# Seven chunks of a layer's matrix products by Strassen's seven products on one Trainium2 core

## The chip, the core and the metric

One NeuronCore of a Trainium2 chip runs the program. Its engines work side by side, each through its own queue in order: TensorE (PE) multiplies matrices into PSUM; VectorE (DVE) and ScalarE (ACT) read PSUM and SBUF; GpSimd (POOL) works on SBUF; SyncE (SP) starts the DMA transfers. They wait for each other through semaphores. The metric is the device time of one execution in microseconds, the median of several runs; lower is better.

## The reference

Two layers over `x` of shape (2, 2048, 512): a conditioned state-space block with a feed-forward part, then attention between two conditioned norms. What matters here, cut from the reference:

```python
# first layer
mod = t @ Wm + bm                      # six rows: shift, scale, gate, twice
y_mod = _ln(y) * (1 + scale_a[:, None]) + shift_a[:, None]
a_y = _s5(y_mod, ...)                  # in-projection, recurrence over L, out-projection
y = y + gate_a[:, None] * a_y
y_norm = _ln(y) * (1 + scale_c[:, None]) + shift_c[:, None]
y_mod = y_norm * (1 + scale_ff[:, None]) + shift_ff[:, None]
h = jax.nn.gelu(y_mod @ W1 + b1)       # 512 -> 2048
ff_y = h @ W2 + b2                     # 2048 -> 512
x = y + gate_ff[:, None] * ff_y
# second layer
h = _sln(x, ...)                       # conditioned layer norm
qkv = h @ Wqkv.T + bqkv                # 512 -> 3 * 512, 16 heads of 32
out = softmax(q k^T) / D**0.5 @ v
h1 = out @ Wp.T + bp + x
return _sln(h1, ...) + h1
```

All arithmetic is in float32.

## The kernel before

The 2 x 2048 rows are cut into eight chunks of 512 rows (`order`). A first stage turns every chunk into x, q, k and v for attention and stores these in DRAM (`x2`, `qd`, `kd`, `vd`); a second stage runs the attention, block by block, from there. Only the first stage is touched by the change, and its two ends.

The order of all work is written out by hand: the engines execute their instructions in the order in which the Python program issues them. For chunk `now` the loop over `f` (16 steps) issues `ff_first` (a block of 128 of the 2048 hidden columns: four float32 matmuls on 128x512 into one PSUM bank, then a gelu on ACT), and one step later `ff_second` (that hidden block times its rows of `w2`, into four accumulating banks, one for each 128 rows of the chunk). Other work is hung between these steps through the dictionary `due`: for the chunk `ahead` its norm (`normalised`), the turning into feature order by 32x32 blocks on DVE and sixteen small DMAs (`by_blocks`), the in-projection, recurrence and out-projection of the state-space block (`s5_in`, `s5_turn`, `s5_scan`, `s5_out`, `s5_direct`), and its second norm (`ff_norm`, `ff_features`); for the chunk `behind` its attention norm (`at_norm`, `at_features`), then q and k (`at_heads`, eight products of 128 columns each, stored in a high and a low half by `halves`) and v (`at_values`). `ff_out` gates the feed-forward's result and adds it to x. A norm is four rows of statistics on DVE (`ln_row`), a chain of twelve small DVE operations (`ln_scale` with `rsqrt`) and four normalising operations (`normalise`).

W1, W2 and the weights of q, k and v lie in SBUF throughout the stage (`w1_sb`, `w2_sb`, `wk`, `wq`, `wv`). PSUM: two single banks for small products (`ones`), two for `ph`, four for `po`. The v of the last two chunks, and q and k of the last, are computed at the start of the second stage (`left`).

## Time and profile before

| what | value |
|---|---|
| median of 3 runs | 3381.46 us (3381.16 to 3383.28) |
| span of the profiled execution | 3379.3 us |
| before the first feed-forward matmul | 0 to 65 us |
| first chunk | 65 to 201.6 us |
| six chunks, each with one ahead and one behind | 164.8 us each |
| last chunk | 137.3 us |
| attention and the end | from 1332.5 us |

The profile is of one execution. A line such as `L538 PE MATMUL ph<-fT,w_sb 128*128 128x512 f32 x1024` gives the line of the code (in a helper where one issues the work), the engine, the output and the inputs by their names, the shapes, how often it occurs, then busy time, mean duration of one and the idle time of the engine before it, with what ended most of that. A float32 matmul of the program appears as two records, for it takes two passes. PEld is the load of a matmul's stationary operand. A mean duration of a matmul includes its way through the array; where matmuls follow each other, the distance of their starts is what each costs. The granted clock (PEclk) is the share of TensorE's full speed.

### The profile page before, as it was taken

How to read it: one execution, taken by the hardware profiler on the slowest of the kernel's cores; microseconds unless marked ns; L12 is line 12 of the kernel's file. 1: busy time of each engine (PE TensorE's matmuls, PEld its weight loads, DVE VectorE, ACT ScalarE, POOL GpSimd, SP SyncE). 2: the span in 40 equal slices, each digit the busy share in tenths (PEclk: the TensorE clock that was granted, in tenths of full speed). 3: DMA queues.
4: the chain of work that ended last, by engine and by line, in shares of the span. 5: the costliest groups of instructions: out<-in, count | busy, mean ns of one | idle time of the engine just before them, and what ended most of it. 6: DMA issues, size and time to landing. Idle time of an engine off the chain costs nothing.

```text
span 3379.3 us, 33635 instructions
## 1 busy us (share of the span) xinstructions
PE 3286.6 (97%) x11076; PEld 1417.1 (42%) x11076; DVE 2218.1 (66%) x2792; ACT 1956.4 (58%) x2210; POOL 2110.7 (62%) x1166
## 2 busy tenths in 40 slices
PE   7999999999999999999999999999999999999996
PEld 4444444444444444444444444434444434444432
DVE  5352525252525211688888888888888888888884
ACT  2111111111111111599999999999889888988962
POOL 2341313131313111399999999989999999999886
PEclk9999999999999999999999999999999999999998
DMA  8022222222222212332313231323233343243233
GB/s 299 25 50 72 53 77 48 78 54 74 62 63 54 59 50 75 106 87 68 74 49 74 68 74 49 74 69 76 67 95 89 68 93 88 61 95 86 62 100 101
DMA packets 249781, 259.07 MB, mean 77 GB/s; under 512 B 94920, under 2 KB 167112, under 8 KB 245510
## 3 DMA queue, kind: packets, MB, share of 16 engines
q1 hardware_dynamic: 249606, 256.92, 29.1%
q8 instruction: 88, 1.44, 0.2%
q14 instruction: 87, 0.71, 0.1%
HBM read 166.77 MB, written 67.76 MB: 69 GB/s over the span
## 4 chain that ended last, share of the span: by engine, by line
PE 62%; ACT 17%; DVE 13%; issue 3%; DMA 2%; POOL 1%; SPq 1%; ACTq 0%; DVEq 0%; POOLq 0%
PE ph L538 13%; PE po L551 13%; PE o L925 10%; PE s L856 8%; DVE run L872 7%; ACT x L867 7%; PE pk L587 7%; ACT x L915 5%; ACT pT L915 4%; PE pv L599 3%; DVE pT L910 3%; PE py L1008 3%; DVE run L876 2%; PE pu L474 2%; PE pt_run L884 1%
## 5 line engine op out<-in xcount | busy, mean ns | idle before, releaser
L904 POOL TENSOR_TENSOR x<-x,shift 128x1024 f32<-128x1024 f32 x704 | 1653.1, 2392 | 131.9 <-DMA shift<-flat 117.0
L856 PE MATMUL s<-qs,ks 128*128 128x512 f32 x2688 | 823.4, 427 | 38.0 <-DVE run L872 25.5
L867 ACT COPY x<-s 128x1024 f32<-128x1024 f32 x704 | 692.0, 1011 | 142.7 <-PE s L856 134.5
L872 DVE TENSOR_TENSOR run<-s,run 128x1024 f32<-128x1024 f32 x576 | 705.0, 1224 | 76.3 <-ACT x L867 31.3
L915 ACT ACTIVATE x<-x 128x1024 f32<-128x1024 f32 x704 | 737.7, 1058 | 18.5 <-POOL x L904 18.2
L925 PE MATMUL o<-x,v 128*64 128x512 f32 x2816 | 717.4, 611 | 0.0
L856 PEld LDWEIGHTS s<-qs,ks 128*128 128x128 f32 x2688 | 444.4, 189 | 452.5 <-DVE run L872 157.2
L538 PE MATMUL ph<-fT,w_sb 128*128 128x512 f32 x1024 | 459.4, 592 | 0.9 <-ACT fT L682 0.9
L551 PE MATMUL po<-w_sb,hid 128*128 128x512 f32 x1024 | 460.0, 592 | 0.0
L542 ACT ACTIVATE hid<-ph,vec 128x512 f32<-128x512 f32 x128 | 87.8, 686 | 615.7 <-PE ph L538 615.7
L910 DVE TENSOR_TENSOR pT<-s,shift 128x1024 f32<-128x1024 f32 x320 | 388.6, 1215 | 51.6 <-PE s L856 51.3
L876 DVE TENSOR_TENSOR run<-s,run 128x1024 f32<-128x1024 f32 x320 | 389.0, 1216 | 9.5 <-PE s L856 9.0
L915 ACT ACTIVATE pT<-pT 128x1024 f32<-128x1024 f32 x320 | 339.4, 1061 | 76.5 <-DVE pT L910 76.1
L561 POOL TENSOR_TENSOR x<-x,gated 128x512 f32<-128x512 f32 x32 | 39.6, 1267 | 506.5 <-DVE gated L560 506.5
L925 PE MATMUL o<-pT,v 128*64 128x512 f32 x1280 | 329.2, 593 | 6.6 <-ACT pT L915 6.6
L164 DVE SCALAR_TENSOR_TENSOR lo<-pk,vec,hi 128x512 fp32r<-128x512 f32 x64 | 47.8, 746 | 422.9 <-ACT hi L163 422.9
L551 PEld LDWEIGHTS po<-w_sb,hid 128*128 128x128 f32 x1024 | 194.5, 190 | 243.9 <-issue 243.4
L538 PEld LDWEIGHTS ph<-fT,w_sb 128*128 128x128 f32 x1024 | 194.1, 190 | 243.3 <-issue 239.1
L925 PEld LDWEIGHTS o<-x,v 128*64 128x64 f32 x2816 | 157.2, 135 | 309.4 <-issue 251.2
L163 ACT ACTIVATE hi<-pk,vec 128x512 fp32r<-128x512 f32 x64 | 44.0, 687 | 373.3 <-PE pk L587 373.3
L524 POOL TENSOR_TENSOR x<-x,gated 128x512 f32<-128x512 f32 x28 | 35.4, 1265 | 255.2 <-DVE gated L523 255.2
L925 PEld LDWEIGHTS o<-pT,v 128*64 128x64 f32 x1280 | 91.4, 137 | 191.3 <-issue 142.5
(281 smaller groups left out, 2446.4 us busy)
## 6 DMA issues: line engine op xcount, KB each, us to landing
ks<-kd SPq DMA_DIRECT2D x128, 256.0 KB
qs<-qd SPq DMA_DIRECT2D x512, 64.0 KB
shift<-flat SPq DMA_DIRECT2D x64, 512.0 KB
moved<-fT SPq DMA_DIRECT2D x224, 64.0 KB
x<-in_x SPq DMA_DIRECT2D x8, 1024.0 KB
w_sb<-in_w SPq DMA_DIRECT2D x8, 1024.0 KB
kd<-hi SPq DMA_DIRECT2D x32, 256.0 KB
kd<-lo SPq DMA_DIRECT2D x32, 256.0 KB
```

Of the source, the lines that this page charges most:

```text
L538: nc.tensor.matmul(ph, w1_sb[:, k, f * P : (f + 1) * P], fts[b, c][:, k, :], start=k == 0, stop=k == KC - 1)
L551: nc.tensor.matmul(pos[b, c][:, t, :], hid[:, t * P : (t + 1) * P], w2_sb[:, f, :], start=f == 0, stop=f == FC - 1,)
L587: nc.tensor.matmul(pk, w[:, k, g * P : (g + 1) * P], hT[:, k, :], start=k == 0, stop=k == KC - 1)
L599: nc.tensor.matmul(pv, fts[b, c][:, k, t * P : (t + 1) * P], wv[:, k, :], start=k == 0, stop=k == KC - 1)
L856: nc.tensor.matmul(s[:, e, :], kst[pair_of[n], e][:, kt * P : (kt + 1) * P], qst[n][:, e, :], start=True, stop=True,)
L867: nc.scalar.copy(x, s)
L872: nc.vector.tensor_tensor(runs[n], s, kept[n, 0] if kt == 1 else runs[n], ALU.max)
L876: nc.vector.tensor_tensor(runs[n], raw_scores(n, kt), runs[n], ALU.max)
L904: nc.gpsimd.tensor_tensor(x, x, shifts[n], ALU.add)
L910: nc.vector.tensor_tensor(x, s, shifts[n], ALU.add)
L915: nc.scalar.activation(x, x, AF.Exp)
L925: nc.tensor.matmul(outs[n][64 * e : 64 * e + 64, :], v[:, kt, e : e + 2, :], x[:, e, :], start=first, stop=final,)
```

## The change

Chunk 0 is computed as before. For chunks 1 to 7 the products of feed-forward (both), of q and k, and of v (chunks 0 to 5, one step behind) are computed by Strassen's scheme in Winograd's form: both operands are cut into 2 x 2 blocks, seven products of blocks take the place of eight, with four sums of blocks of the weights, four of the activations and seven additions of the products.

The weight sums are made during chunk 0 on POOL (`combine`, four operations for each of 22 pieces, each on 128x256) and stored in DRAM with the original blocks that are needed (`w1d`, `w2d`, `wkd`, `wvd`). From then on the weights are streamed: `more` starts the load of the next tile of about 1 MB into a ring of four slots, whose first three are the places of `wk`, `wq` and `wv`. W1 loses its place in SBUF after chunk 0; W2's becomes that of the hidden activations `h1` and `h2`. At the end of the stage the weights of q, k and v are loaded again.

Two procedures issue the products, on 256 moving columns each. `pairs_of` makes the first feed-forward product (eight steps) and q and k (four steps); each step uses one PSUM tile `pp` of two banks, of which there are three:

```python
product(c, ws[c], 0, x11, 0, True, False)
product(c, ws[c], 1, t2, 1, False, False)
product(c, ws[c], 4, t4, 2, True, False)
product(c, ws[c], 2, t1, 3, False, False)
nc.scalar.copy(za[:, 0, :], pps[c][:, 0, :HC])
nc.vector.tensor_tensor(za[:, 0, :], pps[c][:, 0, HC:], za[:, 0, :], ALU.add)
if c:
    product(c - 1, ws.pop(c - 1), 6, x22, 3, False, True)
    more()
    nc.vector.tensor_tensor(za[:, 0, :], pp[:, 1, HC:], za[:, 0, :], ALU.add)
    take(c - 1, 0, 1, za[:, 0, :])
for what, *args in beside.get(2 * c, ()):
    what(*args)
product(c, ws[c], 3, x21, 0, False, True)
product(c, ws[c], 5, t3, 1, True, True)
nc.vector.tensor_tensor(za[:, 1, :], pp[:, 0, HC:], za[:, 0, :], ALU.add)
nc.vector.tensor_tensor(zb, pp[:, 1, :]..., za[:, 1:2, :].to_broadcast([P, 2, HC]), ALU.add)
take(c, 0, 0, pp[:, 0, :HC])
take(c, 1, None, zb...)
for what, *args in beside.get(2 * c + 1, ()):
    what(*args)
```

`whole_of` makes the second feed-forward product (depth 8) and v (depth 2), with two such tiles:

```python
product(0, pa[:, 0, :], True, False)
nc.scalar.copy(u, pa[:, 0, :])
run(0)
product(1, pa[:, 1, :], True, True)
run(1)
nc.vector.tensor_tensor(u, pa[:, 1, :], u, ALU.add)
product(2, pb[:, 1, :], True, False)
run(2)
product(3, pa[:, 0, :], False, True)
run(3)
take(0, 0, pa[:, 0, :])
product(5, pa[:, 1, :], True, True)
run(5)
nc.vector.tensor_tensor(v, pa[:, 1, :], u, ALU.add)
nc.vector.tensor_tensor(z, pb[:, 1, :], v, ALU.add)
take(1, 1, z)
product(4, pb[:, 0, :], True, True)
run(4)
nc.vector.tensor_tensor(v, pb[:, 0, :], v, ALU.add)
take(1, 0, v)
product(6, pb[:, 1, :], False, True)
nc.vector.tensor_tensor(u, pb[:, 1, :], u, ALU.add)
run(6)
take(0, 1, u)
```

`take` hands a finished quarter on: `hidden` (gelu on ACT, and on POOL the sums for the next product), `gated_in` (the first quarter is gated on DVE, the others on POOL, all are added to x on POOL), `heads` (the high and low halves, stored), `values_in` (bias, stored). `beside` and `run` hang the other work between the products, in place of `due`. For the two chunks around it this is, in `pairs_of` for feed-forward:

```python
beside[0] += rows[:2]           # norm of the chunk ahead
beside[1] += rows[2:3]
beside[2] += rows[3:]
beside[3] += scale
beside[4] += to[:2]
beside[5] += to[2:3]
beside[6] += to[3:] + turns[:1]
beside[7] += turns[1:2]
beside[8] += turns[2:] + move
beside[8] += [(s5_direct, *ahead)]
beside[13] += [(s5_features, *ahead, k) for k in range(KC)]
beside[10] += b_rows[:1]        # norm of the chunk behind
beside[11] += b_rows[1:2]
beside[12] += b_rows[2:3]
beside[13] += b_rows[3:]
beside[14] += b_scale
```

`s5_in` and `s5_turn` follow; then in `whole_of`:

```python
beside[0] += [(third,)]
beside[0] += [(s5_scan, *ahead)]
beside[1] += b_to + [(at_rows, *behind)] + b_turns + b_move
beside[2] += [(s5_out, *ahead, t)]            # for each t
beside[3] += [(fourth, 0), (fourth, 1)]
beside[3] += [(at_features, *behind, k) for k in range(KC)]
beside[3] += [(load_x, *order[i + 2])]
beside[3] += rows + scale
beside[5] += to + [(bias, t) for t in range(TT)]
beside[4] += turns + move
beside[4] += [(at_sums, *behind)]
```

`third` (POOL) and `fourth` (DVE) make the last two sums of the hidden activations, `at_sums` (POOL) those for q, k and v, `ff_sums` (DVE) those for the next chunk's first product, at the end of the chunk. In chunk 0 the jobs that make the weight sums stand two to a step from step 3 on; the first three loads of the ring stand at step 13. The accumulator's four banks and `ph`'s two become the three tiles `pp` after chunk 0.

## The prediction

> **What bounds the kernel now.** I read the page's totals and its 40 slices first, then busy time by stretch, then TensorE in order of time, then the groups by shape.

> ```profile
> span 3379.3 us, 33635 instructions
> ...
> PE 3286.6 (97%) x11076; PEld 1417.1 (42%) x11076; DVE 2218.1 (66%) x2792; ACT 1956.4 (58%) x2210; POOL 2110.7 (62%) x1166
> ...
> PEclk9999999999999999999999999999999999999998
> ```

> TensorE is busy nearly throughout, at full clock. The changed stage is slices 3 to 16. Busy time by stretch (start:end, length, then busy us of PE, PEld, DVE, ACT, POOL, granted clock, DMA share, GB/s), the second chunk and the last:

> ```profile
> 201.60:366.40 164.80, 164.80 (x385) 72.88 (x384) 64.27 (x116) 24.92 (x36) 42.97 (x32) 1.00 0.24 64
> ...
> 1195.20:1332.50 137.30, 137.30 (x321) 60.80 (x320) 19.79 (x40) 19.30 (x28) 10.42 (x8) 1.00 0.24 61
> ```

> PE has no gap at all: here a chunk's time is its number of matmul passes times their pitch. The pitch, from the timeline of PE (start, duration, engine, line):

> ```profile
> 390.64 3.60 PE L538 MATMUL ph<-fT,w_sb 128*128 128x512 f32 x8
> 394.08 3.60 PE L551 MATMUL po<-w_sb,hid 128*128 128x512 f32 x8
> ```

> Eight passes in 3.434 us: 0.4292 us for 512 columns. A float32 matmul of the program is two passes; 384 passes make 164.8 us. What shorter passes cost, from the groups by shape:

> ```profile
> L648 PE MATMUL pa_s<-direct,fT 128*128 128x128 f32 x16 | 1.9, 275 | 0.0
> ...
> L1164 PE MATMUL turned<-raw,w 128*128 128x256 f32 x4 | 1.0, 379 | 0.0
> ```

> At 256 columns (1.0 - 0.379)/3 = 0.207, half of 0.4292 is 0.2146: I take 0.215. At 128 columns 1.9/16 = 0.119, each with a weight load of its own, so the load recorded as 190 ns does not hold up a 256-column pass. [...]

> **The change part by part.** *Arithmetic.* A chunk's passes go from 128 + 128 (feed-forward) + 64 (q, k) + 32 (v) = 352 of 512 columns to 224 + 224 + 112 + 56 = 616 of 256: 151.1 - 132.4 = 18.7 us less, for six chunks. In the last chunk, without v, 137.3 - 120.4 = 16.9. In all 129 us, if PE stays gapless.

> *New waits.* It does not. In the built order of the changed program a PSUM pair of banks counts as one tile: a matmul into one bank waits for the last reader of the other. PE is in order, so every product behind it stands too. Durations of what it waits for:

> ```profile
> L137 DVE BATCH_NORM_STATS2 ln_st<-x 128x6 f32<-128x512 f32 x88 | 58.5, 664 | 0.0
> ...
> L126 DVE SCALAR_TENSOR_TENSOR rstd<-rs_b,rstd 128x4 f32<-128x4 f32 x66 | 23.7, 359 | 2.3
> ...
> L560 DVE TENSOR_TENSOR gated<-po,gate_f 128x512 f32<-128x512 f32 x32 | 21.4, 689 | 68.0 <-PE po L551 57.5 <-POOL x L561 10.5
> ...
> L497 DVE TENSOR_TENSOR m<-m,t_im 128x512 f32<-128x512 f32 x7 | 12.2, 1749 | 0.0
> ...
> L484 DVE TENSOR_TENSOR m<-m,m 128x512 f32<-128x512 f32 x7 | 4.8, 682 | 0.0
> ```

> and of ACT, L421 (801 ns) and the copies L604 (585 ns at 512 columns) and L867 (1011 at 1024). By these slopes a 256-column DVE add from PSUM is 0.42, an ACT copy 0.37, a gelu 0.48 (estimates); results follow the last pass by 592 - 429 = 0.16; a hand-over is 0.05. Per chunk:

> - First pairs (eight steps of 28 passes): the product into bank 0 waits for copy and add, 0.16 + 0.37 + 0.42 + 0.15 = 1.1, of which the previous step's last product (0.86) covers all but 0.24: 1.1 + 7 x 0.24 = 2.8. In the last step the copy stands behind four L421 (3.2), about 2.2 net. There too the twelve small operations of a norm's scale (2.35 us from 168.05 to 170.4, where POOL rests; 3.95 by their means, such as L126) stand before the last adds: 2 for them, 2 for add, add and gelu: 4.0. Sum 9.0.
> - Second product (32 passes each): after product 0 an ACT copy, 0.85. Product 5 waits for the gating multiply, which stands on DVE behind the second half of a 128x1024 subtraction (1.2, of which the wait is product 3's end), four norm rows (3.2, as from 85.4 to 88.6) and the scale (2.35): with the multiply and hand-over 7.6; with POOL busy 9.6. Product 4 waits for two adds, 1.6; product 6 for one, 0.95. Sum 11.0.
> - q and k pairs: 1.8 likewise and 2.4 at the end. v, four waits of the second kind, 0.85 + 0.95 + 1.7 + 0.95. Sum 8.7.
> - The next chunk's sums stand behind v's last add on DVE: 0.16 + 0.69 + two at 0.68 (1.7 beside POOL, L497 against L484) less the product that needs none, 0.86: 2.4.
> - Restarts: some 25 a chunk at 0.1 (the first pair of passes after a wait took 1.12 against 1.02). After a gap of 5.9 us at 55 us the clock was 0.58 over the next 5, and sixteen transposes took 3.68 instead of 1.95: so about 2 for the 7.6. Sum 4.5.

> Together 35.6, against 18.7 saved: +16.9 a chunk, 101 for six, less 2.4 since chunk 1 needs no wait for sums. The last chunk has no norms of a next one: 2.8 + 4.0 + 5.6 + 4.2 + 2.4 + 3.3 = 22.3, less 16.9: +5.4. [...]

> *Weights from DRAM.* 21 loads a chunk, 20.2 MB. The stretch 40 to 45 us moved 387 GB/s, so 52 us of some 180, atop a share of 0.24: room. A load is issued when its slot's tile is done and needed three steps (18 us) later; 1 MB at that rate is 2.7. SP issues about 92 DMAs at 0.6 (the block moves' issue). Hidden: 0; if a landing exceeded 18 us, PE would wait for the rest.

> *Chunk 0.* 88 POOL operations on 256 columns, 0.70 each (from 1.27 at 512 and 2.39 at 1024) = 62 us, and 89 DMAs, between L513's end at 108.8 and 202. POOL's own old work there is some 20: it fits barely, and the recurrence's three POOL operations end at 141 to 145, PE needing them at 146.7. Loads of the first tiles queue on SP behind the last sums; and the first pair now waits for all four gatings of the old accumulator (201.8 to 205.8), which the next chunk's matmuls covered. +6, from 3 to 25.

> *The rest.* Adds, gelus, subtractions lie under PE: DVE 64 + 33, POOL 43 + 29, ACT 25 + 9 us a chunk. Attention is untouched; its 3 MB of reloads fall beside the last pairs: 0 (from -3 to +4).

> Sum: 101 - 2.4 + 5.4 + 6 = +110, so 3379.3 + 110 = 3489 for the profiled execution. The median lies 2.2 above that execution: **3492 us**.

> Bounds. Small side: scale at 2.35 and mostly under PE, no clock loss, sums alone, 30 a chunk: +11, 68 + 5 + 3 = 76, 3457. Strided reading by the first pairs' matmuls (runs of 32) no row shows: from 0 to, say, a tenth of 48 us, five a chunk; I take 0, since columns alone set the pitch in every row. Large side: scale and rows beside POOL, stores of q and k late for their two buffers (2 a chunk), 46 a chunk: +27, 164 + 12 + 12 = 188, 3569.

> **Rivals.** *The saving arrives* (the other side). Each of these waits would have to be met early, as all are before: 3379.3 - 129 + 6 = 3256, with the median 3259; it turns faster than before once the gaps of a chunk are under 18.7. For it: DVE has 60% free, and the steps spread the norms by hand. Against: the wait of product 5 alone is ten DVE operations that cannot start before product 3 ends. *The weight stream decides*: if loads came at 110 GB/s beside the small block moves, a chunk would last 20.2/0.11 = 184 us before any DVE wait, and with the non-overlapped half of these about 200: 3381 + 6 x 35 + 15 = 3606. Against: 387 GB/s at 2 KB pieces, and here they are 7 and 8 KB. *Gaps and saving even out*: 18 to 19 us of gaps, 3381 + 6 = 3387.

> **How the numbers follow.** Forecast (waits outweigh the saving) 0.83, stream 0.06, even 0.03, saving arrives 0.08. A measurement here tells 0.2% (6.8 us) from no change. Range 3440 to 3560: the forecast's bounds without their far tails. Faster 0.08, same 0.02, slower 0.90.

> **What would show it.** PE's busy share in a chunk falls from 100% to about 80%, a chunk lasts 180 to 184 us; passes at 0.215; idle of PE put to DVE's gating multiply 7 to 10 us in six places and to ACT's gelu at the end of the first pairs; DMA share near 0.5 without PE waiting for weight tiles. I am wrong if PE stays above 92% in the chunks, if it waits for DMA, or if passes differ from 0.215.

## The result, and the profile after

The changed kernel took 3560.43 us (median of four runs, 3559.02 to 3561.89) against 3381.35 beside it: 1.0526 times as long, 95% interval 1.0512 to 1.0541. The forecast said slower, 3492 us, range 3440 to 3560: the direction was right, and the time lies 0.4 us beyond the upper end of the range. Of a loss of 179 us it named 110.

The page of the changed kernel, its totals and the granted clock in 40 slices:

```profile
span 3559.8 us, 38898 instructions
...
PE 3255.7 (91%) x12900; PEld 1783.0 (50%) x12900; DVE 2393.8 (67%) x3224; ACT 2014.3 (57%) x2391; POOL 2367.1 (66%) x1440
...
PEclk9999999999899999999999999999999999999998
```

TensorE does less (3256 us busy instead of 3287) in a longer span. Busy time by stretch (start:end, length, then busy us of PE, PEld, DVE, ACT, POOL, granted clock, DMA share, GB/s): chunk 0, the second of the six chunks that are alike, the last chunk, its values, the attention:

```profile
65.00:210.07 145.07, 135.35 (x384) 63.19 (x385) 42.16 (x87) 25.33 (x38) 104.89 (x119) 0.98 0.57 177
399.65:588.05 188.40, 158.96 (x649) 125.46 (x648) 88.32 (x178) 33.20 (x62) 70.78 (x59) 0.95 0.52 163
1356.39:1501.00 144.61, 129.01 (x561) 106.53 (x559) 50.85 (x99) 26.57 (x52) 36.91 (x36) 0.98 0.44 149
1501.00:1526.09 25.09, 16.77 (x34) 7.12 (x33) 7.72 (x26) 1.68 (x3) 2.53 (x2) 0.73 0.96 266
1526.09:3559.80 2033.71, 1963.71 (x7772) 817.67 (x7772) 1717.70 (x1753) 1746.11 (x1904) 1784.43 (x897) 0.99 0.31 78
```

The last two stretches of the kernel before, in the same view:

```profile
1332.50:1346.80 14.30, 13.56 (x33) 5.82 (x32) 10.57 (x28) 1.76 (x3) 9.24 (x10) 1.00 0.22 74
1346.80:3379.30 2032.50, 1961.66 (x7774) 817.56 (x7772) 1717.49 (x1753) 1745.36 (x1903) 1781.99 (x896) 0.99 0.31 78
```

The two profiles can be laid side by side by stage. The six chunks ran from 201.60 to 1195.20 before and from 210.07 to 1356.39 after. (Before, that is six times 164.8 us and 4.8 for the gate vectors, 165.6 on the mean.)

| stage | before | after | change | forecast |
|---|---|---|---|---|
| chunk 0 | 136.6 | 145.1 | +8.5 | +6 |
| chunks 1 to 6 | 993.6 | 1146.3 | +152.7 | +98.6 |
| last chunk | 137.3 | 144.6 | +7.3 | +5.4 |
| last chunk's values | 14.3 | 25.1 | +10.8 | 0 |
| attention | 2032.5 | 2033.7 | +1.2 | 0 |
| sum | | | +180.5 | +110 |

So 54 of the missing 70 us lie in the six chunks, 9 in each, and 11 in the values. The second column to read is the clock: 1.00 in every chunk before, 0.95 now. TensorE in order of time around the wait that the forecast called the longest (start, duration, engine, line; in brackets the idle time before it and its releaser):

```profile
508.85 9.96 PE L961 MATMUL pp<-wring,h 128*128 128x256 f32 x32 [7.30 <-DVE gated L1114]
520.32 7.17 PE L961 MATMUL pp<-wring,h 128*128 128x256 f32 x32 [1.51 <-DVE z L987]
528.28 1.99 PE L961 MATMUL pp<-wring,h 128*128 128x256 f32 x8 [0.78 <-DVE v L991]
```

The waits are there and have the forecast sizes: 7.30 for the gating multiply (7.6 forecast), 1.51 and 0.78 for the adds (1.6 and 0.95). What was not expected stands in the second column: product 5's 32 passes last 9.96 us, product 4's, the same work, 7.17. The stretch view (columns as above) over that gap and what follows it:

```profile
501.50:504.20 2.70, 0.05 (x1) 0.00 (x0) 2.58 (x4) 0.58 (x1) 0.00 (x0) 1.00 0.70 126
504.20:514.40 10.20, 5.55 (x13) 4.47 (x14) 8.82 (x23) 2.34 (x4) 5.52 (x4) 0.50 0.69 280
514.40:524.00 9.60, 8.09 (x37) 6.76 (x37) 3.78 (x6) 0.00 (x0) 4.99 (x5) 0.99 0.26 96
```

The clock falls to half 2.7 us into the gap and comes back 10.2 us later, 5.55 us after TensorE has resumed. The forecast had 2 us a chunk for all of this.

How much it is: from L530's first matmul of one chunk to that of the sixth (five chunks) is 958.05 us; less 4.8 for one chunk's gate vectors, 190.65 a chunk. Full-speed work is 616 x 0.2146 + 32 x 0.4292 = 145.9, so 44.7 us a chunk are lost. Recorded gaps in that stretch are 149.1 us, 29.8 a chunk; some 16 results a chunk need 0.17 after the last pass; seven hand-overs of 0.38 lie under the gaps' threshold: 35.2. That leaves 9.5 us. (A pass is one record of the trace; a float32 matmul has two.) The trace's records of the clock place most of it: 18 stretches of half clock lie in the five chunks. The stretch view over these 18 gives the sum (length, then busy us as above):

```profile
sum 105.81, PE 76.37 PEld 54.10 DVE 53.11 ACT 28.90 POOL 24.05; mean PE 4.24 PEld 3.01 DVE 2.95 ACT 1.61 POOL 1.34
```

TensorE works for 76.4 us at half speed and loses half of that, 7.6 us a chunk. The other 1.9 stay open but for 0.8: a run below measures 0.2159 for a pass, not 0.2146.

Two theories were set against each other: A, the missing time is mostly TensorE at half clock after gaps; B, the seven-product form is slow by itself (short passes, strided reads, DMA traffic), and gaps cost their own length only.

### The profile page after: what moved, and what is told of

It reads as the page before. It is cut to its first block, busy times and chain, and to the rows that moved or that the text cites. A ratio compares the mean times of both kernels' runs of the same rounds, so it can differ in the third digit from the quotient of the medians.

```text
span 3559.8 us, 38898 instructions
## 1 busy us (share of the span) xinstructions
PE 3255.7 (91%) x12900; PEld 1783.0 (50%) x12900; DVE 2393.8 (67%) x3224; ACT 2014.3 (57%) x2391; POOL 2367.1 (66%) x1440
## 4 chain that ended last, share of the span: by engine, by line
PE 47%; ACT 17%; DVE 17%; DMA 6%; issue 3%; POOL 3%; SPq 2%; ACTq 0%; DVEq 0%; POOLq 0%
PE pp L961 12%; PE pp L906 10%; PE o L1359 9%; PE s L1290 7%; ACT x L1301 6%; DVE run L1306 6%; ACT x L1349 5%; ACT pT L1349 3%; DVE pT L1344 2%; PE py L1442 2%; POOL x L1338 2%; DMA kd<-hi 2%; DVE run L1310 2%; PE pu L530 1%; PE pt_run L1318 1%
## 5 line engine op out<-in xcount | busy, mean ns | idle before, releaser
L1301 ACT COPY x<-s 128x1024 f32<-128x1024 f32 x704 | 692.3, 1011 | 140.2 <-PE s L1290 131.8
L906 PE MATMUL pp<-fT,wring 128*128 128x256 f32 x1008 | 280.2, 402 | 99.4 <-DVE za L925 48.0
L961 PE MATMUL pp<-wring,h 128*128 128x256 f32 x1344 | 313.1, 393 | 61.9 <-DVE gated L1114 43.8
L906 PE MATMUL pp<-parts,wring 128*128 128x256 f32 x1344 | 327.0, 387 | 13.1 <-DVE parts L875 13.1
L961 PEld LDWEIGHTS pp<-wring,h 128*128 128x128 f32 x1344 | 263.7, 198 | 113.1 <-DVE gated L1114 46.2
L906 PEld LDWEIGHTS pp<-parts,wring 128*128 128x128 f32 x1344 | 260.8, 194 | 52.4 <-DVE parts L875 15.5
L906 PEld LDWEIGHTS pp<-fT,wring 128*128 128x128 f32 x1008 | 189.2, 196 | 162.8 <-DVE za L925 87.2
L924 ACT COPY za<-pp 128x256 f32<-128x256 f32 x84 | 30.9, 368 | 387.7 <-PE pp L906 387.6
L1068 POOL TENSOR_TENSOR h<-h 128x256 f32<-128x256 f32 x56 | 41.7, 745 | 245.7 <-ACT h L1066 233.2
L1203 POOL TENSOR_TENSOR z<-z,bv_row 128x512 f32<-128x512 f32 x6 | 7.6, 1270 | 277.0 <-DVE z L987 277.0
```

Of the source, the lines that this page charges most:

```text
L906: nc.tensor.matmul(to, w[:, m, k, :], moving, start=start and k == 0, stop=stop and k == 1, skip_group_check=True,)
L961: nc.tensor.matmul(out[:, t * HC : t * HC + HC], x(m, q, t), w[:, q, :], start=start and q == 0 and t == 0, stop=stop and q == depth - 1 a ...
L1068: nc.gpsimd.tensor_tensor(h1[:, p, HC:], h1[:, p, HC:], h1[:, p, :HC], ALU.subtract)
L1301: nc.scalar.copy(x, s)
```

## The experiments

All times are medians; "a chunk" is the mean of the five steady ones as above (before 165.8, changed kernel 191.6, with the gate vectors).

**A fill of the longest gap.** Matmuls whose result nobody reads keep TensorE busy while it would stand.

```diff
+    def warm(count):
+        spare = ones.tile([P, CH], F32, name="spare")
+        for _ in range(count):
+            nc.tensor.matmul(spare, ident, bv_row, start=True, stop=True)
...
+        if depth == FH:
+            warm(8)
         product(5, pa[:, 1, :], True, True)
```

> Edit: eight matmuls of 512 columns whose result nobody reads (8 x 0.858 = 6.87 us) go into a bank of their own between products 3 and 5 of the feed-forward's second product, where TensorE stands for 7.30 us in each of seven chunks (six with the norm in the way). Nothing else changes; TensorE only has more to do. Theory A, the clock: what the prediction missed is TensorE at half clock after gaps. The 32 passes of product 5 took 8.56, 9.96, 8.85, 9.77, 8.67 and 9.77 us against 7.07 undisturbed, 13 us in six chunks; filled, they all take 7.07, and the time falls by 10 to 15 us, to about 3547 us. Theory B: the seven-product form is slower of itself (256-column passes, strided reads, weight loads, DMA traffic) and the slow passes after the gap are no matter of the gap: the filled gap costs nothing and gives nothing, 3560 us, or 2 to 4 us more.

Measured: 3556.74 us (ratio 1.0516, 1.0500 to 1.0531), profiled 3552.9. A chunk took 188.8 us, 2.8 less, although TensorE had 6.87 us more to do. TensorE in order of time:

```profile
503.47 7.03 PE L896 MATMUL spare<-bv_row,ident 128*128 128x512 f32 x16
510.93 7.17 PE L966 MATMUL pp<-wring,h 128*128 128x256 f32 x32 [0.43 <-DVE gated L1121]
```

Product 5 takes 7.17 again: the slow passes were a matter of the gap. The total moved by only 3.7 (expected 10 to 15; 6.9 in the profiled execution): chunk 0, which the edit doesn't touch, ended 3.7 us later in this profile, a spread that the profiles of the changed kernel and of its variants show (first pair at 210.1 to 213.8).

**Fills in six gaps of a chunk.**

```diff
+                if (n, c) == (FH, 0):
+                    warm(2)
...
+                if c == n:
+                    warm(3 if n == FH else 2)
                 product(c - 1, ws.pop(c - 1), 6, x22, 3, False, True)
...
+                if (n, c) in ((FH, FH - 1), (KC, KC - 2)):
+                    warm(2)
                 product(c, ws[c], 3, x21, 0, False, True)
```

> Edit: as in the fill of product 5's gap, and in each chunk two such matmuls before the second step of the feed-forward's sums (gap 2.19 us), two before product 3 of the last first pair and three before its last product (gaps 1.64 and 2.92), two before product 3 of the third q/k pair (gap 2.2 to 4.4) and two before the last of these (2.41). Theory A: by chunk, time above the nominal passes was 44 us of which the gaps are 29 and hand-overs 5; the 10 left are half clock. Nearly all of it goes: -50 to -60 us with the first fill's included, 3500 to 3510 us, and the granted clock in a chunk rises from 0.95 to 0.99 or more. Theory B: no gain, and a loss where a fill is longer than its gap, 3560 to 3575 us.

Measured: 3542.63 us (1.0474, 1.0458 to 1.0489): 17.8 less, where A expected 50 to 60 and B none. Stretch view over the five chunks, changed kernel first, then with the fills (columns as before):

```profile
269.34:1227.39 958.05, 805.06 (x3281) 634.09 (x3280) 442.33 (x890) 169.30 (x315) 353.65 (x295) 0.95 0.52 161
```

```profile
272.59:1204.51 931.92, 854.17 (x3472) 650.41 (x3471) 442.15 (x890) 168.86 (x315) 353.38 (x295) 0.99 0.54 165
```

The clock is back at 0.99 with 5.2 us less a chunk. The fills are 19 x 0.858 = 16.3 us a chunk and took away 15.0 of gaps (recorded gaps 149.1 to 74.0): they add 1.3 of their own, so the clock was worth 6.5 a chunk. The clock's records agree: three half-clock stretches are left, 10.2 us, which cost 1.0 a chunk where the changed kernel loses 7.6. B falls: a program that does more on TensorE is faster. A's size was too large because its "10 a chunk" was the whole remainder and the fills' own overhang wasn't subtracted.

**The gating multiply first.**

```diff
-        run(3)
         take(0, 0, pa[:, 0, :])
+        run(3)
         product(5, pa[:, 1, :], True, True)
```

> Edit: the gating multiply that product 5 waits for is issued on VectorE before the second half of the feed-forward's subtraction, the four norm rows and the norm's scale, not behind them. The wait falls from 7.30 to about 1 us; the wait of product 4 for two adds may grow from 1.5 to 2.6, since rows and scale now run into product 5. Theory A: with the gap its half clock goes (2.2 a chunk on the mean): 6 x (5.2 + 2.2) = 44 less, 3516 us. Theory B: the gap alone, 6 x 5.2 = 31 less, 3529 us.

Measured: 3557.91 us (1.0519, 1.0501 to 1.0537), no different from the changed kernel. TensorE, then VectorE, in order of time:

```profile
506.62 7.17 PE L961 MATMUL pp<-wring,h 128*128 128x256 f32 x32 [0.85 <-DVE gated L1114]
520.79 10.08 PE L961 MATMUL pp<-wring,h 128*128 128x256 f32 x32 [7.00 <-DVE z L987]
```

```profile
505.87 0.69 DVE L1114 TENSOR_TENSOR gated<-pp,gate_f 128x512 f32<-128x512 f32 x1 [6.21 <-PE pp L961]
506.48 3.43 DVE L1125 TENSOR_TENSOR h<-h,t 128x1024 f32<-128x1024 f32 x2
...
515.60 3.80 DVE L154 TENSOR_SCALAR xn<-x,mean,rstd 128x512 f32<-128x512 f32 x4 [0.32 <-DVE rstd L133]
519.33 0.68 DVE L986 TENSOR_TENSOR v<-pp,u 128x512 f32<-128x512 f32 x1
520.04 0.69 DVE L987 TENSOR_TENSOR z<-pp,v 128x512 f32<-128x512 f32 x1
```

The wait moved, whole, to the next product: the two adds that product 4 needs now stand behind everything that the multiply stood behind before, subtraction 3.43, rows and scale, and the four normalisations (3.80) that the expectation had left out. VectorE ran its operations in the program's order here too, the two adds last (519.33 and 520.04); taking one operation to the head only changed who waits. The half clock moved along (10.08 for 32 passes).

**One tile for each bank.** The dependence itself is taken away: products 5 and 4 write banks that nobody is reading.

```diff
-        pa = psq.tile([P, 2, CH], F32, name="pp")
-        pb = psq.tile([P, 2, CH], F32, name="pp")
+        pa = [psq.tile([P, CH], F32, name=f"pp{i}") for i in range(2)]
+        pb = [psq.tile([P, CH], F32, name=f"pp{i}") for i in range(2)]
...
-                pps[c] = psq.tile([P, 2, CH], F32, name="pp")
+                pps[c] = [psq.tile([P, CH], F32, name=f"pp{i}") for i in range(2)]
```

> Edit: each pair of PSUM banks that was one tile becomes two tiles of one bank, so a matmul into one bank no longer waits for the reader of the other. Nothing is added or taken away. Of the 29 us of gaps in a chunk the waits for the gating multiply (7.30), for z and v adds (4.6), for gelu (2.9), for the last low half (2.4), for u and the v gating (1.5) and part of those for the copy and add of a first pair (7) are by this false waits of the tile; left are the sums (2.2) and some 4 to 5 of the copies that stand behind ACT's features. Theory A (gaps and their half clock, 10 us a chunk): 33 less a chunk, 3560 - 6 x 33 - 10 = about 3350 us, faster than the kernel before. Theory B (gaps only): 25 less a chunk, about 3400 us, no faster than before. Rival C: VectorE, now with no slack, takes over as the wait and the chunk stays above 180 us.

Measured: 3400.45 us (1.0053, 1.0038 to 1.0068): 160 us less from a change of bookkeeping alone. A chunk took 166.3. TensorE in order of time in the feed-forward's second product:

```profile
468.70 27.79 PE L961 MATMUL pp<-wring,h 128*128 128x256 f32 x128
496.33 1.03 PE L906 MATMUL pp<-fT,wring 128*128 128x256 f32 x4
497.19 2.75 PE L906 MATMUL pp<-parts,wring 128*128 128x256 f32 x12
```

Four products, 128 passes, run without a break in 27.63 us from start to start, 0.2159 a pass; four strided passes (fT) take 0.86, as four of any kind. So the arithmetic of the forecast holds, and in this product the norm operations on VectorE cost TensorE nothing once no tile ties them. At the end of the first pairs, where a norm's scale stands on VectorE ahead of the last adds, they still do:

```profile
433.28 1.13 PE L906 MATMUL pp<-fT,wring 128*128 128x256 f32 x4 [3.08 <-DVE zb L940]
```

The time is the one that B named (about 3400, 25 us less a chunk), but by luck, for B gave all of it to gaps. Recorded gaps fell by 17.1 a chunk (29.8 to 12.7) and half clock by 3.5 (7.6 to 4.1 by its records); the other 4.7, by difference, can be tails and hand-overs. The 3350 that A expected is missed by 50; ACT in order of time shows one part of what stayed:

```profile
508.26 0.47 ACT L170 ACTIVATE hi<-pp,vec 128x256 fp32r<-128x256 f32 x1 [1.27 <-DVE za L939]
514.70 0.72 ACT L170 ACTIVATE hi<-zb,vec 128x512 fp32r<-128x512 f32 x1 [5.96 <-DMA kd<-hi]
515.32 0.35 ACT L924 COPY za<-pp 128x256 f32<-128x256 f32 x1
```

ACT stands 5.96 us for the store of an earlier k tile, and the copy for the next first pair is queued behind it; TensorE then waited 4.56 us for that copy's add. Over the five chunks ACT waited 60 us for k and q stores (41.9 and 18.1) against 38.6 in the changed kernel: the same bytes in less time.

**Three pairs of store tiles, on the changed kernel.**

```diff
-                halves_at[e] = [work1.tile([P, CH], HALF, name=n, tag=n) for n in ("hi", "lo")]
+                by = (strip, ("u", "v")) if (2 * p + e) % 3 == 2 else (work1, ("hi", "lo"))
+                halves_at[e] = [by[0].tile([P, CH], HALF, name=n, tag=tag) for n, tag in zip(("hi", "lo"), by[1])]
```

> Edit: every third pair of tiles that hold q or k before they are stored takes two other free tiles, so three pairs take turns instead of two. Theory A: of the waits in the q and k pairs that the prediction took at 0 (it named 2 us a chunk for late stores), the ones ahead of product 3 (2.2 to 5.2 us a chunk) are ACT standing for a store of an earlier tile, with the copy that TensorE waits for behind it. They go, with their half clock: 3 to 5 us a chunk, 20 to 30 in all, about 3535 us. Theory B: it is the four features that ACT does there, waiting for the block moves: no change, 3558 us or more.

Measured: 3554.96 us (1.0509, 1.0493 to 1.0525), runs from 3551.66 to 3560.15: 5.5 us less where A expected 20 to 30, and hardly beyond the spread of the runs; 2.2 us a chunk in the profile. ACT's waits for k stores fell only in part; the waits of the changed kernel and of this one over the five chunks (waiting engine and line, for whom: total, times, longest):

```profile
ACT hi L170 <- DMA kd<-hi: 27.1, 10, 5.0
```

```profile
ACT hi L170 <- DMA kd<-hi: 16.8, 5, 3.5
```

Stores are a cause of those waits, but one pair more doesn't cover them. How much they weigh in the changed kernel is in its trace, here ACT, then TensorE, in order of time:

```profile
748.11 0.72 ACT L170 ACTIVATE hi<-zb,vec 128x512 fp32r<-128x512 f32 x1 [4.79 <-DMA kd<-hi]
748.73 0.35 ACT L924 COPY za<-pp 128x256 f32<-128x256 f32 x1
```

```profile
750.00 2.07 PE L906 MATMUL pp<-fT,wring 128*128 128x256 f32 x4 [4.21 <-DVE za L925]
```

Ahead of product 3 in the q and k pairs TensorE waits 0.98 in the first step of each chunk, and nine times more, 22.2 us in the five chunks. Each of the nine stands behind a wait of ACT for a k store (1.3 to 5.0 us) as here; in four of them one feature (0.80) lies between.

**The reload as slots come free, on the changed kernel.** The order of the ring's slots changes with it.

```diff
-        if n == total:
-            return
...
+        if n >= total:
+            if tag in sources_of:
+                w = wlate.tile([P, KC, D], F32, name=tag)
+                nc.sync.dma_start(w, sources_of[tag].rearrange("(k p) f -> p k f", p=P))
+                wkqv[tag] = w
+            return
```

> Edit: the three weights that the attention stage reloads are loaded when a slot of the ring of four comes free in the last q/k pairs, not after the last store in SyncE's queue; wv's slot is the first to come free. Expected: the wait of 8.02 us for wv before the last chunk's values goes, with the slow passes behind it (32 passes in 16.76 us against 14): -10 us, 3550 us. If the load is late for another reason (DMA queues full with k and q stores), 3557 us or more.

Measured: 3561.75 us (1.0526, 1.0510 to 1.0542): nothing gained. TensorE in order of time:

```profile
1504.46 14.48 PE L658 MATMUL pv<-wv,fT 128*128 128x512 f32 x32
1524.49 0.76 PE L1290 MATMUL s<-qs,ks 128*128 128x512 f32 x1 [5.55 <-DMA qs<-qd]
```

The 8 us wait for wv is gone and the passes are fast, but behind it lay the attention's own first loads, queued after the last stores and reloads on SyncE: 5.55 us of waiting appear there. The wait for wv had been hiding it.

**Everything together, three times.** Bank tiles, three pairs of store tiles and reload as above, and:

```diff
-            beside[13] += [(s5_features, *ahead, k) for k in range(KC)]
+            for k in range(KC):
+                beside[10 + k] += [(s5_features, *ahead, k)]
...
-        beside[14] += b_scale
+        beside[16] += b_scale
...
-        whole_of(2, weight_v, operand_v, values_in, {})
-        ff_sums(*ahead)
+        whole_of(2, weight_v, operand_v, values_in, {m: [(ff_sums, *ahead)] if m == 4 else [] for m in range(7)})
```

> Edit: one tile for each PSUM bank, three pairs of store tiles, the reload as the slots come free, the next chunk's sums issued on VectorE before v's last two adds, the norm's scale after the last first pair instead of before its adds, and ACT's four features of the s5 stage one to each half step instead of together before the last step's copy. Theory A: of the 13 us of gaps that a chunk has with single-bank tiles 11 go and their half clock (4 us) with them; 3400 - 6 x 15 - 10 = 3300 us (3285 to 3330): the seven products then beat the kernel before by 2%. Theory C: the freed time shows the next queue (ACT or VectorE in order), and the chunk stays at 160 us or above: 3360 to 3380 us.

Measured: 3393.67 us (1.0037, 1.0022 to 1.0051), 165.8 a chunk: theory C of the expectation in kind (the chunk stays above 160), not A; the time lies above C's 3360 to 3380 too. One cause is the edit's own, in ACT's order of time:

```profile
585.23 0.81 ACT L477 ACTIVATE fT<-fT,mod,u_scale 128x512 f32<-128x512 f32 x1 [7.12 <-DMA fT<-turned]
```

The feature was put ahead of the landing of the block move that it reads, and what TensorE needed stood behind it. The second run moved the features later, used four pairs of store tiles and put wq's reload behind the attention's first loads (the two tiles of a pair also got one name with six buffers, in place of two names with three each, and the ring's slots another order; neither was run alone):

```diff
-                beside[10 + k] += [(s5_features, *ahead, k)]
+            for k, at in enumerate((13, 14, 15, 15)):
+                beside[at] += [(s5_features, *ahead, k)]
...
+                by = ((work1, ("hi", "lo")), (work1, ("hi", "lo")), (strip, ("u", "v")), (strip, ("z", "lo0")))[(2 * p + e) % 4]
...
         qst[n] = qs
+        if n == 0:
+            nc.sync.dma_start(wq, w_qT.rearrange("(k p) f -> p k f", p=P))
```

> Edit: as the run with everything together, but ACT's four features of the s5 stage come at the half steps 13, 14, 15 and 15 (at 10 the first of them stood 7.1 us on ACT for a block move that had not landed, and the copy that TensorE waits for stood behind it: a gap of 5.34 us); four pairs of store tiles instead of three; and of the reloads wq's is issued after the first loads of the attention stage (in the run with everything TensorE stood 7.4 us for those). Theory A: the 5.3 us gap with its half clock (2 us) goes in six chunks, some 2 to 4 us of store waits, 5 us before the attention: 3394 - 6 x 9 - 5 = 3335 us (3325 to 3360), faster than before by over 0.6%. Theory C, that with the gaps gone the DMA queues set the time in the q and k pairs (share 0.98 to 1.01 there over 10 us): the store waits stay whatever the number of tiles, and the time is 3350 to 3375 us.

Measured: 3351.28 us (0.9911, 0.9894 to 0.9927), 159.1 a chunk: faster than the kernel before. The time lies in the ranges of both theories and doesn't part them; the waits show what stayed. Waits over its five chunks:

```profile
ACT u L979 <- DMA qd<-hi: 41.9, 5, 8.9
PE pp L966 <- ACT u L979: 26.9, 5, 6.2
```

The borrowed tile u is the one that v's first copy writes, and its store was still under way. The third run deals the tiles out so that u and v are stored from early only:

```diff
+                by = {2: (strip, ("u", "v")), 3: (strip, ("z", "lo0")), 5: (strip, ("z", "lo0"))}
+                by = by.get(2 * p + e, (work1, ("hi", "lo")))
```

> Edit: as the second run with everything, with the store tiles dealt out otherwise. There the sixth pair was stored from the tile that v's first copy writes next, and TensorE stood 20.7 us in four chunks (5.3 in one of them) behind that copy, which waited for the store. Here that tile holds the second pair only, and the last three pairs use the two of their own. Theory A: 4 to 5 us a chunk go, with some half clock: 3351 - 6 x 4.5 = 3324 us (3315 to 3335). Theory C, the DMA queues set the time there whatever the tiles: 3340 us or more.

Measured: 3321.08 us (0.9819, 0.9806 to 0.9832): 1.8% faster than the kernel before, with the same seven products; 153.9 a chunk. Its waits over four chunks, and the stretch view over five (columns as above):

```profile
PE pp L911 <- DVE zb L945: 9.9, 8, 1.2
PE pp L966 <- ACT u L979: 4.2, 4, 1.9
PE pp L911 <- DVE za L930: 4.0, 4, 2.2
```

```profile
262.00:1035.00 773.00, 750.38 (x3291) 620.31 (x3291) 441.67 (x901) 171.61 (x319) 353.57 (x299) 1.00 0.64 200
```

These are 18 us of gaps in four chunks, where the changed kernel has 30 in each one; the mean clock over the five chunks is 1.00. The DMA queues did not set the time (theory C there): the stores are the same, and ACT still waits 18.9 us for q stores in the four chunks, but TensorE's waits behind ACT's copies are down to 8.2 (4.2 and 4.0).

## Why the prediction was right in direction and short in size

- **Arithmetic, -129 us: right.** Without gaps a pass took 0.2159 (0.215 forecast), strided or not (at that figure the saving is 18.1 a chunk, not 18.7). Each of these passes has a weight load of its own: with single-bank tiles the five chunks have 3281 loads to 3282 passes, 629.88 us busy, 0.192 each. From start to start a pass took 0.0013 more than half of a 512-column one (0.4292), so a load can have cost it no more than that.
- **Waits from two banks in one tile: right, and shown.** Gaps, tails and hand-overs come to 35.2 us a chunk against 31.1 + 2.5 forecast; part of that agreement is luck, for the q and k pairs are 3.6 above (below) and the other terms 2 under. Splitting the tiles and changing nothing else took 160 of 179 us away. Product 5's wait was 7.30 (7.6), the first pairs' end 1.64 and 2.92 (2.2 and 4.0), the sums' 2.19 (2.4, which is the middle of what the terms written there give, 1.35 alone and 3.4 beside POOL). The share of TensorE's busy time in the chunks was 84% (805 of 958 us; about 80% forecast).
- **The step that failed: "so about 2 for the 7.6", inside "Restarts ... Sum 4.5".** The clock term was sized from one gap and one recovery. It measures 7.6 us a chunk by the clock's records, and the fills, net of what they add, show 6.5 of it. It is not one gap a chunk that lowers the clock: the five steady chunks have 18 stretches of half clock, some of them after gaps of 2 to 3 us. At 7.6 it alone would have put the forecast 6 x 5.6 = 34 us higher, at 3526.
- **Late stores of q and k, taken at 0 with 2 a chunk as a bound.** The waits of the q and k pairs were forecast at 4.2 and measure 7.8 (5.4 for copies and adds before product 3, that is the nine waits of 22.2 us and five of 0.98 over five chunks, and 2.4 at the end): +3.6. All nine stand behind ACT's waits for k stores, so at most four times 0.80 of the 22.2 are ACT's features. With the clock's 5.6 that is 9.2, where 9 a chunk were missing; the 1.9 that the ledger leaves open and the 2 by which the other waits fell short cancel.
- **"Its 3 MB of reloads fall beside the last pairs: 0".** They were issued behind the last stores in SyncE's queue and cost 8.02 us plus slow passes, 10.8, beyond the forecast's -3 to +4. That TensorE would wait for DMA was one of the prediction's own signs of being wrong. The reload run shows that this is not the reloads' own price: without that wait the attention's loads are late by 5.55 us.
- **Chunk 0, +6: +8.5**, within its bounds of 3 to 25. It is one wait of 8.39 us of the first pair for the old accumulator's gatings, for which the prediction named 201.8 to 205.8: VectorE stood 5.04 us in them for POOL, whose last weight sums ran until 206.8.
- **Weights from DRAM, 0: right** for the weight tiles inside the chunks: no group of waits names them there, at a DMA share of 0.52 (forecast about 0.5).
- **The rivals.** "The saving arrives" was wrong for this program. Its condition, gaps of a chunk below 18.7 us, was not enough: with single-bank tiles alone they are 12.7, and a chunk takes 166.3 against 165.8 before, since tails, hand-overs and half clock are not in it. In the last run, with 18.1 us of gaps in four chunks and the clock at 1.00, the saving arrives, and the time is 60 us below before.

## What to carry to other kernels

When a change puts idle time into an engine that had none, price the clock with it: here each microsecond of gap cost about a quarter of a microsecond more in half-speed passes (7.6 on 29.8), after short gaps (2.92) as well as after long ones (7.30). Ask of every tile that spans two banks whether a writer of the one will wait for a reader of the other; if so, split it before reordering queues, since here a reordering only handed the wait to the next operation in order. A wait that is removed uncovers the next queue: expect a second and third round, and look each time at which transfer holds the tile that the waiting engine wants to write.

## What the runs showed of the hardware

```profile
458.04 1.13 PE L906 MATMUL pp<-fT,wring 128*128 128x256 f32 x4 [2.92 <-ACT h L1066]
...
648.50 2.07 PE L906 MATMUL pp<-fT,wring 128*128 128x256 f32 x4 [2.92 <-ACT h L1066]
650.37 5.64 PE L530 MATMUL pu<-fT,bT_re 128*128 128x512 f32 x8
```

At 458 the four passes take 1.13 us, at 648 the same four take 2.07, and the eight after them 5.64 instead of 3.60. The stretch view over windows of that grid, two around the first place and the one before the drop at the second, tells them apart (columns as above):

```profile
453.08:456.49 3.41, 1.99 (x8) 1.44 (x8) 3.10 (x14) 0.51 (x1) 1.45 (x2) 1.00 0.67 279
456.49:459.91 3.42, 1.87 (x7) 1.29 (x8) 1.32 (x3) 1.25 (x3) 0.00 (x0) 1.00 0.02 5
644.22:647.64 3.42, 1.36 (x7) 0.86 (x5) 3.11 (x11) 0.19 (x1) 1.45 (x2) 1.00 0.49 208
```

At the first place the gap of 2.92 us (455.12 to 458.04) is split between two windows, each with TensorE busy for more than half; at the second (645.58 to 648.50) one window holds 2.06 us of it and only 1.36 us of work, and at its end the clock falls. Over the five chunks, the 17 full-clock windows that end in a drop have TensorE busy for at most 0.40 of them, the 232 that don't for at least 0.45; half clock ended after windows at least 0.82 busy and went on after those of at most 0.75.
